# Two transformer layers on one core: gene products of two tiles side by side, two dense steps moved ahead of the experts, and unit-matrix products before the first rows

## The chip, the cores and the metric

The kernel runs on one core of one Trainium2 chip. A core has five engines with a queue of instructions each: TensorE (PE; its weight loads are listed as PEld), VectorE (DVE), ScalarE (ACT), GpSimd (POOL) and SyncE (SP, which here only issues transfers). Within a queue instructions start in order; between queues they wait on semaphores. TensorE writes its products to PSUM, here in banks of 128 partitions by 512 float32; [...] transfers (DMA) move data between SBUF and HBM.

The metric is the time of one execution on the device in microseconds, and of several executions the median.

## The reference

The input x has 4 batches of 512 rows of 256 features, all float32. Two layers follow one another. Each normalises x over the features and adds two branches to it.

Layer 0, branch one, is a linear attention: q, k and v are projections, phi(z) = elu(z) + 1, a running sum over the rows of phi(k) * v is multiplied by phi(q), and a projection closes. Branch two is the gene layer. In short:

```
logits  = (rms_norm(x) * norm_w) @ Wc.T / temperature      # 512 genes per row
w       = softmax of the 32 largest logits
expressed = sum over those 32 of w * genes[index]          # 32 numbers per row
down    = tanh(expressed @ Wd.T);  up = expressed @ Wu.T   # 256 each
branch  = down * rms_norm(x) * up * scale
```

Layer 1, branch one, is an attention with exp(k) weights and running sums over the rows, followed by a gated layer of width 1024. Branch two is a mixture of 16 experts of width 176: two experts are chosen for every row, and a shared gated layer of width 352 is added.

## The kernel before

**Tiles and stages.** A tile is 128 rows; a batch has 4 tiles, all together 16. The stages are written as Python generators, and the helper `together` takes pieces of several of them in turn. The order within the program's queues is then fixed when the program is built: a scheduler goes through the pieces and may move an instruction ahead of others on its engine.

- `layer0(b, i0, nt)` does layer 0 of `nt` tiles of batch b. The batches come as (0; 2 tiles), (0; 2 tiles), (1; 4), (2; 4), (3; 4).
- `mix(b, i0, nt)` does layer 1's attention up to the running sums and the choice of experts.
- `dense(busy)` does the gated layers of layer 1 (width 352 and 1024) for half batches: 8 halves of 11 chunks each, so 88 steps. A step is one `up` (L584, 4 matmuls) and, two steps later, its `down` (L604, 2 matmuls). ScalarE takes a tanh of the gate (`th`, L588), VectorE multiplies (L590, L592). In the first four halves the last multiplication is on GpSimd (L595).
- `route` works out the rows' places per expert, `scatter` sends the 2048 x 2 chosen rows to a buffer in HBM sorted by expert (32 indirect transfers on POOL, L552), `experts` fetches the sorted rows (L720), transposes them (L712), and computes 42 tiles with their expert's weights (L749, L770) in 21 pairs.
- At the end 32 indirect transfers on POOL bring each row's two results back (`ys`, L885), and VectorE adds them to x (L896).

**Dense steps as filling.** 44 of the 88 steps run together with layer 0 and the mixing. Then come 5 with `route`, 14 with `scatter`, a rest before the experts, `run_all(islice(dd, 2 * NC - 19))` with NC = 11, so 3 steps, and the remaining 22 after the experts, together with the gathers. The scatters and gathers carry an extra dependence on the last `down` product written so far (`paced`, `beat`), so that they spread over the dense steps. In the loop after the experts a gather with number `asked` is issued from the step with 5 * asked <= 9 * step on, and an addition with number `added` from 17 * added <= 32 * (step - 3) on.

**The gene branch of a tile** in `layer0`: `logits` (L296, two matmuls of 128x512), a copy to SBUF (L300), `top` on VectorE (four rounds of MAX8 and MATCH_REPLACE, L308 and L309, and the sum L316) which leaves the unscaled weights `e`, and `express`: four transposes of `e` (L323), a copy on ScalarE (`wT`, L325), four matmuls with 32 columns of genes each that write partial sums to four groups of 32 partitions (L328), a copy (`exT`, L329), one matmul with all 128 rows against `wdut`, which holds the weights of down and up four times below one another (L331, result `du`), tanh on ScalarE (L333), one product on VectorE (L336) and four operations on GpSimd (L338 to L341). At the end of `layer0`, `out` projects the attention (L346) and adds it (L349). Every product of `layer0` and `mix` takes one of four PSUM banks in turn (`bank()`).

**The start.** The unit matrix `ident` and `ones` are made on POOL (L107 and L109), transfers bring x of batch 0 and the weights, VectorE multiplies `wct` by `norm_w` (L157) and takes statistics (L208 to L215) and normalised rows (L220). The first products of TensorE are the transposes of these rows (L228).

Of the kernel before, what the change touches and what calls it, by code (L numbers as in the profile page):

```python
# [11 lines left out]
F32 = mybir.dt.float32  # L12
AF = mybir.ActivationFunctionType
ALU = mybir.AluOpType
AX = mybir.AxisListType

P = 128
B, L, D = 4, 512, 256
NT = L // P
NH = D // P  # L20
NG, GD, NACT = 512, 32, 32
NGC = NG // P
# [5 lines left out]
NTT = B * NT  # L28
# [10 lines left out]
def run_all(steps):  # L39
    for _ in steps:  # L40
        pass
# [13 lines left out]
def tile_two_layers(  # L55
# [24 lines left out]
    V, S, G, T = nc.vector, nc.scalar, nc.gpsimd, nc.tensor  # L80
# [12 lines left out]
    def paced(inst):  # L93

        tc.add_manual_dep(
            inst,
            beat[-1],
            mybir.DependencyInfo(mybir.DependencyClass.Sync, mybir.DependencyReason.DATA),
            reason="transfers spread over the dense parts",
        )  # L100
        return inst
# [4 lines left out]
    ident = const.tile([P, P], F32, name="ident")  # L106
    make_identity(nc, ident)  # L107
    ones = const.tile([P, L], F32, name="ones")
    G.memset(ones, 1.0)  # L109

    load_x(0)
    wqkv = wp.tile([P, NH, 3 * D], F32, name="wqkv")
    wct = wp.tile([P, NH, NG], F32, name="wct")
    nc.sync.dma_start(wct, wc.rearrange("(h p) g -> p h g", p=P))
    nwc = wp.tile([P, NH], F32, name="nwc")
# [6 lines left out]
    gn = wp.tile([P, NGC, GD], F32, name="gn")  # L122
    nc.sync.dma_start(gn, genes.rearrange("(c p) k -> p c k", p=P))

    wdut = wp.tile([P, 2 * D], F32, name="wdut")
# [28 lines left out]
    bqkv1 = wp.tile([P, 4], F32, name="bqkv1")  # L154
    V.tensor_scalar(bqkv1, bqkv[:, 0:4], 1.0, None, ALU.add)
    for h in range(NH):
        V.tensor_scalar(wct[:, h], wct[:, h], nwc[:, h : h + 1], None, ALU.mult)  # L157
    rtemp = wp.tile([P, 1], F32, name="rtemp")
    V.tensor_scalar(rtemp, tmp1, 0.1, None, ALU.max)
    V.reciprocal(rtemp, rtemp)  # L160
# [25 lines left out]
    ps_a = ctx.enter_context(tc.tile_pool(name="ps_a", bufs=1, space=bass.MemoryType.PSUM))  # L186
# [5 lines left out]
    io = first.enter_context(tc.tile_pool(name="io0", bufs=2, side="right"))  # L192
    one = first.enter_context(tc.tile_pool(name="one0", bufs=1, side="right"))

    def bank():
        return ps_m.tile([P, L], F32, name="pm")


    carry = wk.tile([P, 6], F32, name="carry")
# [31 lines left out]
    def layer0(b, i0, nt):  # L231
# [56 lines left out]


        rden = io.tile([P, NT], F32, name="rden")  # L290
        exT = one.tile([P, L], F32, name="exT")

        def logits(i):
            pl = bank()
            for h in range(NH):
                T.matmul(  # L296
                    pl, xnT[:, h, i * P : (i + 1) * P], wct[:, h], start=(h == 0), stop=(h == NH - 1)
                )
            lg = io.tile([P, NG], F32, name="lg")
            S.copy(lg, pl)  # L300
            return lg

        def top(i, lg):
            tp = io.tile([P, NACT], F32, name="top")
            rep = io.tile([P, NG], F32, name="rep")
            for r in range(NACT // 8):
                src = lg if r == 0 else rep
                V.max(tp[:, 8 * r : 8 * r + 8], src)  # L308
                V.match_replace(rep, tp[:, 8 * r : 8 * r + 8], src, TAKEN)  # L309
                if r == 0:  # L310
                    nm = io.tile([P, 1], F32, name="nm")
                    V.tensor_scalar(nm, tp[:, 0:1], sl[:, 0, i : i + 1], -1.0, ALU.mult, ALU.mult)
                    e = io.tile([P, NG], F32, name="e")
                    S.activation(e, lg, AF.Exp, bias=nm, scale=sl[:, 0, i : i + 1])
            den = io.tile([P, 1], F32, name="den")
            V.scalar_tensor_tensor(e, rep, TAKEN, e, ALU.is_equal, ALU.mult, accum_out=den)  # L316
            V.reciprocal(rden[:, i : i + 1], den)
            return e

        def express(i, e):  # L320
            pw = bank()
            for c in range(NGC):
                T.transpose(pw[:, c * P : (c + 1) * P], e[:, c * P : (c + 1) * P], ident)  # L323
            wT = io.tile([P, NGC, P], F32, name="wT")
            S.copy(wT.rearrange("p c t -> p (c t)"), pw)  # L325
            px = bank()
            for c in range(NGC):
                T.matmul(px[c * GD : (c + 1) * GD, 0:P], gn[:, c], wT[:, c], start=True, stop=True)  # L328
            S.copy(exT[:, i * P : (i + 1) * P], px[:, 0:P])  # L329
            du = bank()  # L330
            T.matmul(du, exT[:, i * P : (i + 1) * P], wdut, start=True, stop=True)  # L331
            dn = io.tile([P, D], F32, name="dn")
            S.activation(dn, du[:, 0:D], AF.Tanh, scale=rden[:, i : i + 1])  # L333
            cf = io.tile([P, 1], F32, name="cf")
            V.tensor_tensor(cf, rden[:, i : i + 1], sl[:, 1, i : i + 1], ALU.mult)
            V.scalar_tensor_tensor(dn, du[:, D : 2 * D], cf, dn, ALU.mult, ALU.mult)  # L336
            xw = io.tile([P, D], F32, name="xw")
            G.tensor_tensor(xw, xn[:, i], nwb, ALU.mult)  # L338
            G.tensor_tensor(dn, dn, xw, ALU.mult)
            G.tensor_tensor(xs[:, b, i0 + i], xs[:, b, i0 + i], bob, ALU.add)  # L340
            G.tensor_tensor(xs[:, b, i0 + i], xs[:, b, i0 + i], dn, ALU.add)  # L341
# [9 lines left out]

        parts = [lambda h=h, f=f: f(h) for h in range(NH) for f in (attend_kv, attend_q)]
        lg = logits(0)
        for i in range(nt):
            nxt = logits(i + 1) if i + 1 < nt else None
            e = top(i, lg)
            yield
            for part in parts[i * len(parts) // nt : (i + 1) * len(parts) // nt]:
                part()
            yield  # L360
            express(i, e)
            lg = nxt
            yield
        for i in range(nt):
# [206 lines left out]
    NC = len(chunks)  # L571
# [61 lines left out]
    dd = dense(4)  # L633
# [4 lines left out]
    def a(b, i0, nt):  # L638
        return layer0(b, i0, nt), 2 + 4 * nt
# [45 lines left out]
    routing.close()  # L685
    together((scatter(), 33), d(14))

    run_all(islice(dd, 2 * NC - 19))

    held = ctx.enter_context(ExitStack())  # L690
    wx = held.enter_context(tc.tile_pool(name="wx", bufs=2))
# [188 lines left out]
    added = 0  # L880
    for step, _ in enumerate(dd):
        while asked < 2 * NTT and 5 * asked <= 9 * step:
            n, k = divmod(asked, 2)
            paced(
                G.indirect_dma_start(  # L885
                    out=ys[:, asked],
                    out_offset=None,
                    in_=yrows,
                    in_offset=bass.IndirectOffsetOnAxis(ap=slot[:, k, n : n + 1], axis=0),
                ).ins  # L890
            )
            asked += 1
        while added < 2 * NTT and 17 * added <= 32 * (step - 3):
            n, k = divmod(added, 2)
            here = xs[:, n // NT, n % NT]
            V.scalar_tensor_tensor(here, ys[:, added], cpair[:, k, n : n + 1], here, ALU.mult, ALU.add)  # L896
            added += 1
            if added % 4 == 0 and added < 2 * NTT:
                b, i = divmod(n - 1, NT)
                nc.sync.dma_start(  # L900
                    out[b, i * P : (i + 2) * P].rearrange("(t p) d -> p t d", p=P), xs[:, b, i : i + 2]
                )
# [60 lines left out]
```

## Time and profile before

| what | value |
|---|---|
| runs of the kernel | 581.03, 581.01 and 578.38 us, median 581.01 |
| profiled execution, its own time | 576.85 us |
| span of the profiled execution, first to last instruction | 575.1 us |
| mean granted TensorE clock | 0.976 |
| PE busy | 527.4 us (92%) |
| DVE busy | 370.3 us (64%) |
| ACT busy | 228.4 us (40%) |
| POOL busy | 173.6 us (30%) |
| first TensorE product (L228) | 9.32 us |
| last scatter issued (L552), first fetched rows used (L712) | 396.26 us, 401.66 us |
| last VectorE sum of the dense part | 569.70 us |

The page gives shares over the whole span; the stages differ, and what bounds each of them has to be read from that stretch. A matmul in float32 is listed as two records. Records overlap: a record of 128x256 is listed with 0.38 us, but records start 0.216 us apart when nothing hinders them, and it is these starts that count. Idle time in brackets stands before an instruction, with what ended it. A granted clock of 0.5 means that TensorE works at half speed.

### The profile page before, as it was taken

Reading aid. Unit: us, or ns where it says so; the run is one execution under the profiler, and the core shown is the slowest. Engines: PE = TensorE matmul, PEld = TensorE weight load, DVE = VectorE, ACT = ScalarE, POOL = GpSimd, SP = SyncE. Lnnn points to the kernel's source line nnn. Section 1 sums busy time; section 2 is a strip of 40 time slices with the busy share of each in tenths; the row PEclk is TensorE's granted clock in tenths of the full one; section 3 lists DMA queues with packets and bytes.
Section 4 is the critical chain, followed back from the end, with each engine's and each line's share of the span. In section 5 each row is a group of like instructions: output and inputs, shape, how many; then the busy total and the mean of one; then the engine's idle time right before and its main releaser. Section 6 shows DMA issues by size and latency. Waiting matters only on the chain.

```text
span 575.1 us, 7191 instructions
## 1 busy us (share of the span) xinstructions
PE 527.4 (92%) x2324; PEld 383.5 (67%) x2324; DVE 370.3 (64%) x985; ACT 228.4 (40%) x517; POOL 173.6 (30%) x214
## 2 busy tenths in 40 slices
PE   3557989989999999999999989997999999999996
PEld 1344656558656676566677768886677777788885
DVE  4979999998796797967981499232222222236653
ACT  1452746562655825458344611111433333321110
POOL 1235132354222423223352322774000000016660
PEclk9788899999999999999999999999899999999999
DMA  5995000000000000000045630233333332114441
GB/s 165 376 375 206 1 1 0 2 0 1 0 2 0 0 1 2 0 1 1 1 144 158 202 100 11 103 109 126 94 110 101 102 109 92 55 66 129 123 143 40
DMA packets 37736, 46.76 MB, mean 81 GB/s; under 512 B 3936, under 2 KB 34240, under 8 KB 37440
## 3 DMA queue, kind: packets, MB, share of 16 engines
q1 hardware_dynamic: 34624, 37.87, 20.2%
q0 software_dynamic: 3072, 8.39, 4.8%
q8 instruction: 20, 0.33, 0.2%
q14 instruction: 20, 0.16, 0.1%
HBM read 27.64 MB, written 18.61 MB: 80 GB/s over the span
## 4 chain that ended last, share of the span: by engine, by line
PE 54%; DVE 22%; POOL 8%; ACT 7%; issue 4%; DMA 4%; SPq 0%; POOLq 0%; ACTq 0%; DVEq 0%
PE gu L584 12%; PE pu L749 9%; PE acc L604 7%; PE py L770 6%; PE pm L391 5%; DVE rep L309 4%; DVE top L308 4%; POOL xrows L552 3%; PE pt L712 3%; POOL ys L885 3%; PE pm L251 3%; PE pm L296 2%; PE pm L228 2%; PE pm L346 2%; DVE sums L437 2%
## 5 line engine op out<-in xcount | busy, mean ns | idle before, releaser
L584 PE MATMUL gu<-yT,wugt 128*128 128x256 f32 x512 | 126.0, 381 | 0.0
L584 PEld LDWEIGHTS gu<-yT,wugt 128*128 128x128 f32 x512 | 94.9, 190 | 18.9 <-issue 7.2
L588 ACT ACTIVATE th<-gu 128x256 f32<-128x256 f32 (+1 forms) x88 | 33.5, 382 | 122.7 <-PE gu L584 116.1
L885 POOL DMA_INDIRECT ys<-yrows,slot x32 | 30.7, 961 | 133.4 <-PE gu L584 117.9
L604 PE MATMUL acc<-wot,hid 128*128 128x256 f32 x256 | 66.2, 381 | 0.4
L595 POOL TENSOR_TENSOR hid<-hid,th 128x256 f32<-128x256 f32 (+1 forms) x44 | 34.1, 779 | 101.2 <-ACT hid L594 97.9
L590 DVE SCALAR_TENSOR_TENSOR th<-th,gu 128x256 f32<-128x256 f32 (+1 forms) x88 | 36.1, 412 | 41.6 <-ACT th L588 41.5
L749 PE MATMUL pu<-wex,xgT 128*128 x168 | 58.3, 470 | 0.8 <-DMA xg<-xrows 0.8
L604 PEld LDWEIGHTS acc<-wot,hid 128*128 128x128 f32 x256 | 48.1, 190 | 9.3 <-POOL hid L595 2.0
L251 PE MATMUL pm<-xnT,wqkv 128*128 128x512 f32 (+1 forms) x120 | 46.7, 530 | 3.9 <-ACT qk L398 1.7
L584 PE MATMUL gu<-xn1T,sgu 128*128 128x256 f32 (+1 forms) x192 | 47.3, 382 | 1.4 <-ACT hid L594 1.3
L758 DVE TENSOR_TENSOR hb<-pu,hb 128x176 f32<-128x176 f32 x42 | 14.3, 341 | 51.9 <-ACT hb L757 51.9
L391 PE MATMUL pm<-w,xn1T 128*128 128x512 f32 (+1 forms) x128 | 45.9, 502 | 0.1
L584 PEld LDWEIGHTS gu<-xn1T,sgu 128*128 128x128 f32 (+1 forms) x192 | 33.8, 181 | 9.5 <-ACT hid L594 2.6
L770 PE MATMUL py<-wex,hgT 128*128 x168 | 39.8, 379 | 0.0
L391 PEld LDWEIGHTS pm<-w,xn1T 128*128 128x128 f32 x128 | 24.7, 194 | 21.7 <-issue 17.5
L251 PEld LDWEIGHTS pm<-xnT,wqkv 128*128 128x128 f32 x120 | 23.8, 201 | 21.9 <-issue 13.2
L770 PEld LDWEIGHTS py<-wex,hgT 128*128 128x128 f32 x168 | 31.8, 190 | 7.9 <-issue 0.4
L552 POOL DMA_INDIRECT xrows<-xn,slot x32 | 30.9, 966 | 19.7 <-DVE th L590 10.3
L749 PEld LDWEIGHTS pu<-wex,xgT 128*128 128x128 f32 x168 | 29.4, 195 | 10.5 <-ACT xgT L726 1.2
L762 DVE COPY hgT<-pt 128x512 f32<-128x512 f32 x21 | 14.5, 691 | 30.0 <-PE pt L712 30.0
L296 PE MATMUL pm<-wct,xnT 128*128 128x512 f32 x64 | 33.4, 659 | 0.3 <-ACT xnT L244 0.2
(163 smaller groups left out, 872.2 us busy)
## 6 DMA issues: line engine op xcount, KB each, us to landing
xrows<-zero SPq DMA_DIRECT2D x1, 6016.0 KB, 23.3
wex<-in_w_gate_up_dram SPq DMA_DIRECT2D x8, 704.0 KB, 4.7
xg<-xrows SPq DMA_DIRECT2D x21, 256.0 KB, 2.7
yrows<-yg SPq DMA_DIRECT2D x21, 256.0 KB, 2.1
xs<-in_x_dram SPq DMA_DIRECT2D x4, 512.0 KB, 8.0
wugt<-in_wug_dram SPq DMA_DIRECT2D x1, 2048.0 KB, 11.9
wex<-in_w_down_dram SPq DMA_DIRECT2D x4, 512.0 KB, 4.8
out_dram<-xs SPq DMA_DIRECT2D x7, 256.0 KB, 2.8
```

Source lines behind the costliest of these rows:

```text
L251: T.matmul(pm, wqkv[:, h, c * P : (c + 1) * P], xnT[:, h, 0:W], start=(h == 0), stop=(h == NH - 1),)
L296: T.matmul(pl, xnT[:, h, i * P : (i + 1) * P], wct[:, h], start=(h == 0), stop=(h == NH - 1))
L391: T.matmul(o[:, 0:n], xnT[:, h, i * P : (i + 1) * P], w1[:, h, at : at + n], start=(h == 0), stop=(h == NH - 1),)
L552: sc = G.indirect_dma_start(out=xrows, out_offset=bass.IndirectOffsetOnAxis(ap=slot[:, k, i : i + 1], axis=0), in_=xn1[:, i // NT, i % NT] ...
L584: T.matmul(gu[0:m, k], w[:, h, at : at + m], ins[which][:, h], start=(h == 0), stop=(h == NH - 1))
L588: S.activation(th[0:m], gu[0:m, 0], AF.Tanh, scale=0.5)
L590: V.scalar_tensor_tensor(th[0:m], th[0:m], 1.0, gu[0:m, 0], ALU.add, ALU.mult)
L595: G.tensor_tensor(hid[0:m], hid[0:m], th[0:m], ALU.mult)
L604: mm = T.matmul(acc[:, t], hid[0:m, t * P : (t + 1) * P], dw[0:m, dc], start=(n == 0 and t == 0), stop=(n == NC - 1), skip_group_check=True,)
L749: T.matmul(pg[:, 0 : 2 * NI], xT[:, i, h], wex[:, bass.ds(at[i] + h * 2 * NI, 2 * NI)], start=(h == 0), stop=(h == NH - 1),)
L770: mm = T.matmul(py[:, i * D : (i + 1) * D], hT[:, i, h], wex[:, bass.ds(at[i] + EW - (2 - h) * D, D)], start=(h == 0), stop=(h == 1),)
L885: G.indirect_dma_start(out=ys[:, asked], out_offset=None, in_=yrows, in_offset=bass.IndirectOffsetOnAxis(ap=slot[:, k, n : n + 1], axis=0) ...
```

## The change

There are five edits, and a number in the tail that goes with one of them.

1. **Gene products in pairs.** `express` is cut into three. `turn_genes(e)` transposes and copies the weights of a tile. After every second tile `express(i, wTs)` multiplies both tiles' weights with the genes: the first tile takes two groups of 32 partitions, the second the other two, and each group adds up two chunks of genes (8 matmuls for the pair, as before). One copy takes the result of both. Then two matmuls follow, one for each tile, each with half of the 128 rows and a bank of its own. `expressed` is the part behind them, once per tile.
2. **Dense steps.** `2 * NC - 17` takes the place of `2 * NC - 19`: five steps run between scatters and experts, and 20 remain behind the experts. For those, 15 takes the place of 17 in the condition for an addition.
3. **Unit-matrix products.** Sixteen products of `ident` with itself are put at the head of TensorE's queue. They write to the bank of the dense sums, and nothing reads them.
4. **`ones`** is filled by VectorE, not by GpSimd.
5. **`wct`** is multiplied by `norm_w` on GpSimd, not on VectorE.

```diff
-    G.memset(ones, 1.0)
+    V.memset(ones, 1.0)
...
-        V.tensor_scalar(wct[:, h], wct[:, h], nwc[:, h : h + 1], None, ALU.mult)
+        G.tensor_scalar(wct[:, h], wct[:, h], nwc[:, h : h + 1], None, ALU.mult)
...
+    idle = ps_a.tile([P, 2, D], F32, name="acc")
+    for _ in range(16):
+        T.matmul(idle[:, 0, 0:P], ident, ident, start=True, stop=True)
...
-        exT = one.tile([P, L], F32, name="exT")
...
-        def express(i, e):
+        def turn_genes(e):
             pw = bank()
             for c in range(NGC):
                 T.transpose(pw[:, c * P : (c + 1) * P], e[:, c * P : (c + 1) * P], ident)
             wT = io.tile([P, NGC, P], F32, name="wT")
             S.copy(wT.rearrange("p c t -> p (c t)"), pw)
+            return wT
+
+        def express(i, wTs):
             px = bank()
-            for c in range(NGC):
-                T.matmul(px[c * GD : (c + 1) * GD, 0:P], gn[:, c], wT[:, c], start=True, stop=True)
-            S.copy(exT[:, i * P : (i + 1) * P], px[:, 0:P])
-            du = bank()
-            T.matmul(du, exT[:, i * P : (i + 1) * P], wdut, start=True, stop=True)
+            for c in range(2):
+                for g in range(NGC):
+                    j = g % 2 * 2 + c
+                    T.matmul(
+                        px[g * GD : (g + 1) * GD, 0:P], gn[:, j], wTs[g // 2][:, j], start=(c == 0), stop=(c == 1)
+                    )
+            exT = io.tile([P, P], F32, name="exT")
+            S.copy(exT, px[:, 0:P])
+            dus = [bank(), bank()]
+            for t, du in enumerate(dus):
+                half = slice(t * P // 2, (t + 1) * P // 2)
+                T.matmul(du, exT[half], wdut[half], start=True, stop=True)
+            for t, du in enumerate(dus):
+                expressed(i + t, du)
+
+        def expressed(i, du):
             dn = io.tile([P, D], F32, name="dn")
...
+        wTs = []
         for i in range(nt):
...
-            express(i, e)
+            wTs.append(turn_genes(e))
+            if len(wTs) == 2:
+                express(i - 1, wTs)
+                wTs = []
...
-    run_all(islice(dd, 2 * NC - 19))
+    run_all(islice(dd, 2 * NC - 17))
...
-        while added < 2 * NTT and 17 * added <= 32 * (step - 3):
+        while added < 2 * NTT and 15 * added <= 32 * (step - 3):
```

## The prediction

> **What bounds the kernel now.** I read four views: the page for the whole, the busy times by stretch, the waits of each engine, and the timeline around the places that the diff touches. The page first: busy tenths of the two busiest engines and the granted TensorE clock, in 40 slices of 14.4 us.
>
> ```profile
> PE 527.4 (92%) x2324; PEld 383.5 (67%) x2324; DVE 370.3 (64%) x985; ACT 228.4 (40%) x517; POOL 173.6 (30%) x214
> ...
> PE   3557989989999999999999989997999999999996
> ...
> DVE  4979999998796797967981499232222222236653
> ...
> PEclk9788899999999999999999999999899999999999
> ```
>
> TensorE (PE) is full from the fifth slice on, with one dip in slices 27 and 28. Before that VectorE (DVE) is the full one. The busy times by stretch (length, then busy us of PE, PEld, DVE, ACT, POOL, granted clock) put numbers on it:
>
> ```profile
> 14.92:54.16 39.24, 25.76 (x92) 15.52 (x90) 34.73 (x109) 15.62 (x33) 15.43 (x21) 0.78 0.97 350
> 54.16:86.00 31.84, 26.16 (x116) 16.59 (x116) 31.38 (x97) 19.31 (x44) 6.31 (x10) 0.95 0.00 1
> 86.00:141.00 55.00, 53.08 (x231) 34.27 (x231) 53.87 (x146) 30.59 (x67) 23.64 (x30) 1.00 0.00 1
> 141.00:224.70 83.70, 81.20 (x363) 56.21 (x362) 68.25 (x174) 45.01 (x99) 24.77 (x31) 1.00 0.00 1
> 224.70:297.50 72.80, 70.80 (x303) 46.99 (x302) 62.13 (x156) 37.54 (x87) 25.27 (x27) 1.00 0.02 6
> ...
> 397.68:407.13 9.45, 4.89 (x14) 3.25 (x14) 0.94 (x3) 2.21 (x4) 0.00 (x0) 0.64 0.52 153
> ```
>
> Until 54 us DVE is busy 34.7 of 39.2 us and TensorE runs at 0.78 of its clock; to 86 us DVE is the bound; to 141 us both are; from there to 297 us PE is, with some 4.5 us idle. The 9.45 us from 397.68 are the one hole. The timeline of that seam between scatters and experts (start, us, engine):
>
> ```profile
> 396.82 1.03 PE L604 MATMUL acc<-wot,hid 128*128 128x256 f32 x4
> ...
> 398.81 8.65 SPq L720 DMA_DIRECT2D xg<-xrows  x6
> ...
> 401.66 1.09 PE L712 MATMUL pt<-ident,xg 128*128 128x128 f32 x4 [3.81 <-DMA xg<-xrows]
> 402.86 0.58 ACT L726 COPY xgT<-pt 128x512 f32<-128x512 f32 x1 [5.46 <-PE pt L712]
> 403.46 1.28 ACT L757 ACT_TABLE_LOAD   x1
> ...
> 403.50 2.71 PE L749 MATMUL pu<-wex,xgT 128*128 x4 [0.75 <-DMA xg<-xrows]
> ```
>
> The last dense product streams until 397.68, the expert's rows arrive at 401.66, and the work behind that runs at half clock. Last, the gene products of one tile in the PE timeline (L328 genes, L331 down and up), and where DVE starts in earnest:
>
> ```profile
> 98.10 0.43 PE L328 MATMUL pm<-wT,gn 128*32 128x128 f32 x8
> 98.46 0.70 PE L584 MATMUL gu<-yT,wugt 128*128 128x256 f32 x2
> 98.99 1.04 PE L331 MATMUL pm<-wdut,exT 128*128 128x512 f32 x2
> ...
> 14.92 0.69 DVE L308 MAX8 top<-lg 128x8 f32<-128x512 f32 x1 [2.88 <-ACT lg L300]
> ```
>
> [...] the four column tiles of L328: they start within 0.02 us of each other (278.595 to 278.615), and some 0.09 us pass unused on either side. No row tile is in this trace. [...] 0.5 is recorded from 400.30 to 407.13, and transposes start 0.213 us apart instead of 0.109.
>
> **Seam and tail.** Two dense steps go from behind the experts to before them. A step is 12 records 0.216 us apart, 2.59 us; two are 5.18. Their operands are ready, and they add no transfer. They run from 397.68 to 402.86, over the 3.98 us of idle; that the experts then start 1.2 us after their rows costs nothing, as the same 5.18 us are gone from the tail. Gain 3.98. The clock also stays up: eight transposes give back 8 x 0.104 = 0.83 us and four L749 records 4 x 0.291 = 1.16, some 2.0. I give back 0.4, because the 1.28 us table load behind the copy at 402.86 then ends after the first L749 pair instead of under it. Seam: -5.6 (ends -4.0, idle alone, and -6.0).
>
> In the tail 20 steps remain, with gathers asked at the old rate (9 in 5 steps) and additions faster (32 in 15 steps, not 17). The last gather is asked at step 18 as before, but its addition, formerly at step 20 of 22, now also belongs to step 18 of 20, and the built order of DVE ends: th of step 19, last addition, hid of step 19. Call E the end of the down product of step 16. In the trace the last gather starts 0.27 us after it (560.17, 560.44), and its addition 2.88 us later (563.32): E+3.15. Hid then ends at E+3.97, and the last down product starts near E+4.05; unhindered it would start after up(19), down(17) and down(18), at E+3.29. Tail: +0.75 (0.4 to 1.5). A gather 1 us slower adds 1 us. Earlier additions wait too, but hid has a step to spare there.
>
> **Front.** Sixteen unit-matrix products, 32 records, start once the unit matrix is made (near 1.9 us; the mask on POOL ends at 1.79). Cold they take 32 x 0.213 = 6.8 us, to 8.7, before the first rows are wanted (9.32): they cost nothing. If the clock rises, the first four transposes take 0.44 instead of 1.14 us and the first pair of logits products (four records) 1.73 instead of 3.4. The two products on wct leave DVE (0.88 us at 6.55), but DVE still waits for the temperature until 7.97, so only some 0.35 us come of it. On POOL they are bounded by twice its memset of 128x512 (2 x 0.53) and four times a 128x256 TENSOR_TENSOR (4 x 0.73); [...] wct and norm_w have landed by 6.4 us, so POOL ends by 7.5 to 9.4, and the logits start near 10: hidden by that transpose and copy. Each us later would delay all logits by one. The memset of ones costs DVE nothing, idle until 4.32. So the first MAX8 starts near 12.6 instead of 14.92: 2.3 us.
>
> How much lasts? From 14.92 to 54.16 DVE idles 4.5 us: 1.94 and 0.36 for tanh, 0.87 for phi, 0.91 for POOL. In the built order the two gene tails come late, behind statistics of the next batches, whose x lands at 31.7 and 33.2 us: about 1.2 us of new waiting, then 1.7 for POOL, which has both tiles' four operations in a row. That leaves 1.2 us saved, so up to 3.5 in all. I take -2.5 (ends 0, if those waits eat it, and -4.5).
>
> **Gene products.** Per pair of tiles before: two column blocks of 0.45 us and two L331 products of 2 x 0.43: 0.9 + 1.73. After: one block of eight matmuls, four rounds, about 0.69 us if whole; the built order splits five of the eight into 2 and 6 (drained twice, about 1.12). Over the six pairs of the dense stages, four split, that is a loss of about 0.5 us. The two L347 products take half the rows each and a bank each: 0.86 + 0.19 us of drain if side by side, saving 0.68 a pair, 4.1 in six; 1.73 + 0.19 if in turn, losing 1.1. One exT copy of 0.27 us a pair leaves ACT and one of two waits for it leaves PE, some 0.8 us in all. Side by side this is -4.4, in turn +0.8 to +1.6. Where DVE is bound as well (to 141 us) it is worth less: I take -2.5.
>
> **Sum.** -5.6 + 0.75 - 2.5 - 2.5 = -9.85 us on a profiled execution of 576.85 (span 575.1 and 1.75 around it): 567.0. The median of the runs shown, 581.01, lies 4.2 us above that execution; I carry this offset over: 571.2.
>
> **The rivals.** (1) Only the dense move counts: row tiles go in turn or PE waits for DVE, and the front's gain is lost in DVE's order. Then -5.6 + 0.75 gives 576.2. For it: DVE is 98% busy from 54 to 141 us. Against: the 2.88 us before the first MAX8 are plain PE time. (2) The change does not do what it says at the tail: gathers slower than 2.88 us hold the last hid, and what the seam won returns. At 4 us more, with rival 1, 580.2. Against: the last five gathers reached their addition in 2.78 to 2.91 us. (3) Slower: a pair needs three of the four banks together, each du held until DVE's dn has read it, and PE, in order, stands at the second L347 with projections and dense products queued behind it; DVE waits for those in turn. It decides from about 1.2 us a pair (8 pairs, 9.85); at 1.7 us it gives 584.8. For it: dn stood behind other DVE work for up to 2.3 us (281.10 to 283.40). Against: PE waited for dn only twice in 30 to 345 us, 1.9 us.
>
> **How the numbers follow.** About 0.5%, 2.9 us, is what a measurement tells from no change. All parts as reckoned: 0.62, 571.2, its own range 568 to 574. More than that, near 567: 0.06. Rival 1: 0.20, 576.2. Rival 2: 0.06. Rival 3: 0.06. Faster takes the first two and nearly all of rival 1, 0.86; within 0.5% rival 2 and the rest, 0.08; slower 0.06. The range of 8 in 10 runs from 566 (both part gains at their ends) to 577 (rival 1 and some noise).
>
> **What would show it.** Right: PE without a gap before the first pt, clock 1.0 there; L347 records of a pair starting within 0.02 us, du block near 1.05; first MAX8 near 12.6; last hid waiting for a gather, PE idle under 1 us. Wrong: L347 records 0.43 us apart for all four; PE idle before the second of a pair or before the last acc; logits waiting for POOL. The forecast fails most easily in the front and the genes, whose PE time may turn into waiting for DVE.

## The result, and the profile after

The changed kernel took 575.82 us in the median (573.79 to 577.93), against 580.15 us for the kernel before (578.38 to 581.52) in the same set of runs: a ratio of 0.9931, with a 95% interval of 0.9913 to 0.9948. That is 4.3 us, where the forecast had 9.85. The profiled execution has a span of 573.6 us.

The page of the changed kernel, the rows that answer to those shown of before:

```profile
PE 530.2 (92%) x2356; PEld 388.5 (68%) x2356; DVE 368.4 (64%) x984; ACT 226.6 (40%) x509; POOL 173.3 (30%) x215
...
PE   8547899989999999999999989879999999999995
...
DVE  6969999998896897968952687223322222225553
...
PEclk9767999999999999999999999979999999999998
```

Before, the dip of PE stood in slice 28 (7 tenths; the prediction put it at 27 and 28). It is gone, and a new one stands in slices 26 and 27, with the granted clock down in slice 27. The seam itself is as forecast, in the PE timeline of the changed kernel (start, us, engine):

```profile
404.97 1.03 PE L628 MATMUL acc<-wot,hid 128*128 128x256 f32 x4
405.83 0.60 PE L736 MATMUL pt<-ident,xg 128*128 128x128 f32 x4
407.19 1.16 PE L773 MATMUL pu<-wex,xgT 128*128 x3 [0.75 <-ACT xgT L750]
```

No gap stands ahead of L736, and its four transposes, one record each, take 0.60 us in place of 1.09. But they start at 405.83 us, 4.2 us later than before, although two steps of 2.59 us ahead of them account for 5.2 and the first scatter came 5.3 us earlier. The time went between the first and the last scatter: 39.4 us in the first profile of the kernel before (356.89 to 396.26), 44.7 in this one (351.58 to 396.26). The waits of the changed kernel from 352 to 400 us show where (waiting instruction, what ended it, us in total, times, longest):

```profile
ACT th L612 <- PE acc L628: 8.7, 2, 5.3
...
PEld acc L628 <- DVE xs L639: 6.0, 1, 6.0
PE acc L628 <- DVE xs L639: 5.6, 1, 5.6
ACT th L612 <- remote: 5.0, 2, 3.9
```

ScalarE's tanh is late by several us in the middle of the scatters; VectorE, which needs it, and then TensorE stand. The same list for the first profile of the kernel before has no wait of PE at all there. I call this the hold: ScalarE's tanh comes late again and again among the scatters, and the other engines wait behind it. The question was then whether the change makes it.

### The profile page after: what moved, and what is told of

The parts are those of the page before. It is cut to its first block, busy times and chain, and to the rows that moved or that the text cites. A ratio compares the mean times of both kernels' runs of the same rounds, so it can differ in the third digit from the quotient of the medians.

```text
span 573.6 us, 7243 instructions
## 1 busy us (share of the span) xinstructions
PE 530.2 (92%) x2356; PEld 388.5 (68%) x2356; DVE 368.4 (64%) x984; ACT 226.6 (40%) x509; POOL 173.3 (30%) x215
## 4 chain that ended last, share of the span: by engine, by line
PE 48%; DVE 27%; issue 8%; POOL 6%; DMA 4%; ACT 4%; SPq 1%; POOLq 0%; another core or an unknown queue 0%; ACTq 0%; DVEq 0%
PE gu L608 11%; PE pu L773 9%; PE py L794 6%; PE acc L628 6%; POOL ys L909 5%; DVE rep L313 5%; DVE top L312 4%; PE pm L415 4%; PE pt L736 3%; DVE sums L461 3%; DMA wot<-in_wout_dram 2%; DVE sums L452 2%; PE pm L256 2%; PE pm L233 2%; DVE th L614 2%
## 5 line engine op out<-in xcount | busy, mean ns | idle before, releaser
L608 PEld LDWEIGHTS gu<-yT,wugt 128*128 128x128 f32 x512 | 96.2, 192 | 20.9 <-issue 8.8
L773 PE MATMUL pu<-wex,xgT 128*128 x168 | 56.9, 461 | 0.8 <-ACT xgT L750 0.8
L773 PEld LDWEIGHTS pu<-wex,xgT 128*128 128x128 f32 x168 | 28.6, 190 | 10.1 <-ACT xgT L750 1.0
L618 ACT COPY hid<-gu 128x256 f32<-128x256 f32 (+1 forms) x44 | 16.4, 373 | 42.4 <-DVE th L614 42.0
```

What stands on the lines that cost most here:

```text
L608: T.matmul(gu[0:m, k], w[:, h, at : at + m], ins[which][:, h], start=(h == 0), stop=(h == NH - 1))
L773: T.matmul(pg[:, 0 : 2 * NI], xT[:, i, h], wex[:, bass.ds(at[i] + h * 2 * NI, 2 * NI)], start=(h == 0), stop=(h == NH - 1),)
```

## The experiments

A set of runs stays on one chip and has runs of the kernel before in it. The sets turned out to be of two kinds, so that each is named by its chip: on A the kernel before took 580.26 us, on B 576.76 and 576.91 (two sets), on C 576.21, on D 576.22.

### Both kernels once more (chip A)

Both kernels are unchanged.

> The changed kernel once more, for a second profile. In its first profile the 32 scatters took 44.7 us from the first start to the last (39.4 in the kernel before), with the tensor engine idle for about 5.6 us in between, and that ate the 5.3 us which were won ahead of them. Theory 'the stall belongs to the order of work': it is there again, at the same scatters, 44 to 45 us, and the span is again about 573.6. Theory 'the stall is a chance event of one execution': the scatters take 39.4 to 39.7 us, and the span is 568 to 569 in this profile; the median of the timed runs is then made up of executions with and without it.

> The kernel before once more, for a second profile. Its first profile took 576.85 us by its own time, less than any of its 11 timed runs (578.38 to 581.52). Theory 'the first profile was a lucky execution': this one is about 580 by its own time, and some stage of it, the scatters being the first suspect, is 2 to 4 us longer than in the first. Theory 'profiled executions are as a rule shorter than timed ones': again about 577.

Measured: the changed kernel 575.64 us, ratio 0.9914 (0.9886 to 0.9942); the kernel before 581.09 us in its profiled execution. The kernel before has the hold too: 43.8 us from first to last scatter, as the changed kernel has (43.7). Its ScalarE timeline, second profile:

```profile
365.74 0.38 ACT L588 ACTIVATE th<-gu 128x256 f32<-128x256 f32 x1 [2.21 <-issue]
371.63 0.38 ACT L588 ACTIVATE th<-gu 128x256 f32<-128x256 f32 x1 [5.51 <-PE gu L584]
...
386.11 0.38 ACT L588 ACTIVATE th<-gu 128x256 f32<-128x256 f32 x1 [6.00 <-PE acc L604]
393.88 0.94 ACT L588 ACTIVATE th<-gu 128x256 f32<-128x256 f32 x3 [7.39 <-remote]
```

and its PE timeline:

```profile
388.43 1.89 PE L584 MATMUL gu<-yT,wugt 128*128 128x256 f32 x8
395.23 2.08 PE L604 MATMUL acc<-wot,hid 128*128 128x256 f32 x4 [4.92 <-DVE hid L592]
```

An undisturbed step has its tanh every 2.59 us (2.21 of idle). Here single ones come after 5.9, 6.4 and 7.8 us, and TensorE stands for 4.92 us shortly before the last scatters. At the seam it then has no gap: the late dense steps fill the time until the expert's rows are there. So the change does not make the hold, and it was the first profile of the kernel before that had none. The theory "chance event of one execution" falls as well: the hold is there in every profile from this chip.

### Dense move undone, genes undone (chip A)

```diff
-    run_all(islice(dd, 2 * NC - 17))
+    run_all(islice(dd, 2 * NC - 19))
...
-        while added < 2 * NTT and 15 * added <= 32 * (step - 3):
+        while added < 2 * NTT and 17 * added <= 32 * (step - 3):
```

> The changed kernel with the dense move undone (17 steps are left behind the experts in place of 15, two fewer ahead of the first rows; the adds again at 17). My forecast prices the move at -5.6 at the seam and +0.75 in the tail, so this should be slower than the changed kernel by about 4.9 us (3.4 to 5.6): about 580.7. If the seam's idle is no longer there, because the stage ahead ends later for another reason, it is within 1.5 us of the changed kernel.

Measured: 576.78 us, ratio 0.9953 (0.9935 to 0.9970), about 1.1 us over the changed kernel of the same set, as the second branch of the expectation has it. The first rows are used 3.9 us earlier than in the changed kernel (402.24 against 406.16) and the end comes 0.5 us later (span 574.7 against 574.2): what two steps more ahead of the experts cost there, they give back behind. With the hold there is hardly a gap for them to fill: even without them TensorE waits for only 0.60 us ahead of the first transposes.

For the genes, `express`, `exT` and the loop are taken from the kernel before:

```diff
-            wTs.append(turn_genes(e))
-            if len(wTs) == 2:
-                express(i - 1, wTs)
-                wTs = []
+            express(i, e)
```

> The changed kernel with the gene products one tile at a time, as before. Forecast: the pairs are worth 2.5 us (4.4 if they run side by side), so this is 578.3 to 580.2. The milestones of the changed kernel's trace (third stage of the first layer 2.2 us earlier, fourth 1.9) say 4 us, so 579.8. If what is won there is lost again in the scatters, then it is 575.8, and its scatters take less than 44.7 us.

Measured: 578.87 us, ratio 0.9990 (0.9963 to 1.0017), 3.2 us over the changed kernel. Its runs spread from 576.23 to 583.87 us, four of the twelve above 581.7, so the 3.2 is rough. The last theory of that expectation falls: the time is not 575.8, and the scatters take 43.9 us, no less than the changed kernel's 43.7 on this chip.

### Single parts, and the scatters (chip B)

First the dense move alone, on the kernel before; its diff is the one above, turned round.

> The kernel before with the dense move alone (two more steps ahead of the first rows, adds at 15). My forecast: -5.6 at the seam and +0.75 in the tail, -4.85, so 575.3 against a median of 580.2. New theory, from the second profile of the kernel before: as a rule the tensor engine is held for 4 to 5.6 us in the middle of the scatters, which leaves nothing to fill at the seam (gap ahead of the first rows under 0.8 us, not 4); then the move is worth -1.0 as in the changed kernel (0 to -1.5): 579.2, and the profile shows the hold near the 12th scatter and no gap at the seam.

Measured: 571.14 us against 576.76, ratio 0.9904 (0.9887 to 0.9921). On this chip no profile has the hold: the scatters take 39.4 us. The old forecast held (-4.85; measured -5.6 in the medians), the new theory, which made the hold a rule, did not.

```diff
-    V.memset(ones, 1.0)
+    G.memset(ones, 1.0)
...
-        G.tensor_scalar(wct[:, h], wct[:, h], nwc[:, h : h + 1], None, ALU.mult)
+        V.tensor_scalar(wct[:, h], wct[:, h], nwc[:, h : h + 1], None, ALU.mult)
...
-    idle = ps_a.tile([P, 2, D], F32, name="acc")
-    for _ in range(16):
-        T.matmul(idle[:, 0, 0:P], ident, ident, start=True, stop=True)
```

> The changed kernel with its front undone: no unit-matrix products, ones set on GpSimd, wct scaled on the vector engine. Forecast: the front is worth 2.5 us (0 to 4.5), so 578.3. From the profiles (at the first scatter the changed kernel with genes one by one is 1.6 us ahead of the kernel before): 577.4. From the sum of what the other two undone parts cost (1.0 and 3.0 of 4.3): only 0.3, so 576.1.

Measured: 569.47 us, ratio 0.9869 (0.9849 to 0.9889). The expected figures in us belong to a kernel before of 580.2 and do not fit here; against the changed kernel on the same chip (567.41, next set) taking the front away costs 2.1 us, or 1.7 by the ratios, whose intervals just overlap.

In the next kernel 24 of the 32 scatters are left out, so that those rows of the experts' input stay zero:

```diff
             for i in range(NTT):
+                if k * NTT + i >= 8:
+                    yield
+                    continue
                 sc = G.indirect_dma_start(
```

> The changed kernel with 24 of its 32 scatters left out (those rows of the expert input stay zero, and the output is wrong by that). If the scatters cause the hold of the activation engine, which in every disturbed profile begins when the 10th scatter starts: the steps of the dense part run every 2.59 us from 350 to 400, the tensor engine has no gap over 1 us there, and the end is 4 to 6 us earlier (568 to 570). If it comes from the dense part itself, from instruction loading or from the recording: a hold of about 5.6 us near 371 as before.

Measured: span 565.4 us, no hold. Without a hold on this chip to begin with, it says nothing of its cause. It does say that without a hold the scatters no longer bound the changed kernel: with a quarter of them the time from the first scatter to the end is 213.6 us, with all of them 213.1.

And the scatters laid over 17 steps:

```diff
-    together((scatter(), 33), d(14))
+    together((scatter(), 33), d(17))
...
-    run_all(islice(dd, 2 * NC - 17))
+    run_all(islice(dd, 2 * NC - 20))
```

> The changed kernel with the 32 scatters spread over 17 dense steps in place of 14, and as many steps ahead of the experts in all (three fewer between the last scatter and the first rows). A scatter comes every 1.38 us in place of 1.26. If the hold comes from the rate at which the scatters are issued, it shrinks, and PE's gap goes to the seam: 573 to 576. If it comes after a number of scatters, whatever their rate: it is there again at the 10th to 12th, and with it the scatters end 3 us later, which opens a gap of up to 3 us at the seam: 576 to 579.

Measured: 568.10 us, ratio 0.9854 (0.9835 to 0.9872); the last scatter starts 39.9 us after the first in place of 39.5, and no gap opens. The edit hardly did what was expected of it: in the trace the scatters from the second to the 16th still start 1.26 to 1.27 us apart, and the later ones 1.26 and 1.33 in turn, where 1.38 was expected. So nothing is learnt of the hold, and this version could not have told a rate from a number at the 10th scatter even where the hold is.

### The changed kernel without the hold (chip B again)

> The changed kernel once more. In the runs so far the kernel before took 580.2 wherever the profiles had the hold among the scatters, and 576.8 where they had none, and its first profile (576.85) had none. So: if the kernel before takes about 576.8 here, no hold, the last scatter near 391.2, and the changed kernel is 8.7 us faster (front 1.2 to 2.5, genes 2 to 3, dense move 5.6 less 0.5): 567 to 569. If it takes about 580.2 here, the hold is there and the changed kernel is again at 575 to 576.5.

Measured: 567.41 us (566.61 to 567.83) against 576.91, ratio 0.9840 (0.9822 to 0.9857), so 9.5 us faster. The stretch from 370 to 380 us (length, busy us of PE, PEld, DVE, ACT, POOL, granted clock), in this profile of the changed kernel:

```profile
370.00:380.00 10.00, 10.00 (x48) 8.64 (x47) 3.64 (x9) 1.53 (x4) 7.63 (x8) 1.00 0.30 105
```

and in the first one, with the hold:

```profile
370.00:380.00 10.00, 4.42 (x13) 3.26 (x12) 3.13 (x7) 1.15 (x3) 6.13 (x7) 0.73 0.23 79
```

TensorE is busy all the time in the one, for 4.42 of 10 us and at 0.73 of its clock in the other. It is the same program.

> The kernel before with the dense move alone, once more. Where the kernel before takes 580.2 (the hold is there): 579.2, the move worth -1.0 (0 to -1.5), where my forecast said -4.85 and the run with a kernel before of 576.8 gave -5.6. Where it takes 576.8: again -5.6.

Measured: 571.25 us, ratio 0.9910 (0.9892 to 0.9927): 5.2 us faster in ratio, as without the hold before.

> The changed kernel with the scatters spread over 17 steps, once more. Where the kernel before takes 580.2: if the hold depends on the rate of the scatters, 572 to 574, less than the changed kernel; if it comes after ten scatters whatever the rate, 575 to 578. Where it takes 576.8: the same as the changed kernel within 1 us.

Measured: 567.80 us, ratio 0.9852 (0.9832 to 0.9873), the same as the changed kernel.

In the next kernel every second scatter is left out:

```diff
             for i in range(NTT):
+                if i % 2:
+                    yield
+                    continue
                 sc = G.indirect_dma_start(
```

> The changed kernel with every second scatter left out (those rows of the expert input stay zero, and the output is wrong by that), so that 16 are issued, about one in 2.6 us. Where the kernel before takes 580.2: if what holds the activation engine fills up at the rate of the scatters and drains in between, no hold at all; if it is a number of scatters, the hold begins at the 10th of these, about 24 us after the first. Where it takes 576.8: no hold, and nothing is learnt.

Measured: span 565.1 us, no hold on this chip.

### The parts once more (chip C)

> The changed kernel with the dense move undone, once more. Where the kernel before takes 576.8 (no hold among the scatters): the move is worth 4.85 by my forecast, 5.6 by its run alone, so 567.4 + 4.9 to 5.6 = 572.3 to 573.0, and the gap ahead of the first rows is back (about 4 us). Where it takes 580.2: 1 us over the changed kernel, as in its first run.

Measured: 573.58 us, ratio 0.9951 (0.9935 to 0.9967), so 6.4 us of the 9.2 that the changed kernel's ratio gives on this kernel before go with the dense move, somewhat more than the 4.9 to 5.6 expected. The gap is back, in the PE timeline of this kernel:

```profile
392.55 1.03 PE L628 MATMUL acc<-wot,hid 128*128 128x256 f32 x4
397.54 1.08 PE L736 MATMUL pt<-ident,xg 128*128 128x128 f32 x4 [3.97 <-DMA xg<-xrows]
399.38 2.71 PE L773 MATMUL pu<-wex,xgT 128*128 x4 [0.75 <-DMA xg<-xrows]
```

and the changed kernel without the hold, in the same view:

```profile
397.33 1.03 PE L628 MATMUL acc<-wot,hid 128*128 128x256 f32 x4
398.20 0.60 PE L736 MATMUL pt<-ident,xg 128*128 128x128 f32 x4
399.55 1.45 PE L773 MATMUL pu<-wex,xgT 128*128 x4 [0.75 <-ACT xgT L750]
```

This is the forecast's seam line by line: 3.97 us of idle gone, transposes 0.60 in place of 1.08 us, four L773 records 1.45 in place of 2.71. The granted clock is 1.00 from 390 to 410 us, where without the dense move it is 0.79 to 400 us and 0.87 from there.

> The changed kernel with the gene products one tile at a time, once more. Without the hold: forecast 2.5, so 569.9; by the gap between the runs of the changed kernel (-9.5) and what the front undone (2.1) and the dense move (4.9 to 5.6) leave: 1.8 to 2.5, so 569.2 to 569.9. With the hold: 3.0 over the changed kernel, as in its first run.

Measured: 571.07 us, ratio 0.9917 (0.9891 to 0.9942), 4.4 us over the changed kernel by the ratios (0.9917 less 0.9840). Expected were 1.8 to 2.5. At the first scatter the profile lies 2.1 us behind the changed kernel (354.31 against 352.24); another 2.0 us come in the tail, where a gather is late, VectorE's sum with it, and PE waits for the bank:

```profile
PE acc L609 <- DVE xs L620: 2.2, 1, 2.2
```

That wait (2.1 us on chip A) is 0.38 us in the changed kernel's third profile.

> The changed kernel with the scatters over 17 steps, for a third time. Where the kernel before takes 580.2: if the hold depends on the rate, 572 to 574; if not, 575 to 578. Without the hold it is the changed kernel within 1 us (two runs so far: 568.1 and 567.8 against 567.4).

Measured: 568.04 us, ratio 0.9857 (0.9833 to 0.9880). Three runs of this version have given the changed kernel's time; it is not a better one.

> The changed kernel with every second scatter left out, once more (the output is wrong by those rows). Where the kernel before takes 580.2: if what holds the activation engine fills up at the rate of the scatters and drains in between, no hold; if it is a number of scatters, the hold begins at the 10th of these, about 24 us after the first. Without the hold nothing is learnt.

Measured: span 564.7 us, no hold here either.

### More unit-matrix products (chip D)

```diff
-    for _ in range(16):
+    for _ in range(26):
```

> The changed kernel with 26 unit-matrix products in place of 16. The 16 end 0.6 to 2.0 us before the first transpose, and in three of ten profiles the tensor engine's clock was halved for 3.4 us from 10.4 to 10.6 on, with the first MAX8 near 14.6 in place of 12.6. Ten more products of 0.11 us (at the full clock) bridge that. If the front's worth hangs on the clock there: the first MAX8 always near 12.6 to 13.2, and 0.3 to 0.7 us less in the median, ratio 0.983 where the kernel before takes 576.8. If the lost time is made up by the end of the first stage anyway (there the same profiles were 2.2 to 2.4 us ahead, as the others): no difference, ratio 0.984 (0.9925 where the kernel before takes 580.2).

Measured: 570.64 us, ratio 0.9898 (0.9880 to 0.9916), so about 3.3 us slower than the changed kernel; both expectations missed. In the first profile of the changed kernel the records of these products come to start 0.111 us apart, and a product is two records: by that ten more take some 2.2 us, where the expectation has 0.11 a product. The first MAX8 is at 13.52 us, a little above the 12.6 to 13.2 of the first expectation, and then 3 us are lost in ScalarE's queue. Its timeline in this kernel:

```profile
23.52 0.59 ACT L329 COPY wT<-pm 128x512 f32<-128x512 f32 x1 [4.15 <-PE pm L327]
30.00 0.63 ACT L672 ACTIVATE wot<-wot 128x512 f32<-128x512 f32 x1 [5.90 <-DMA wot<-in_wout_dram]
30.54 0.46 ACT L269 ACTIVATE phi<-pm,nbqk 128x256 f32<-128x256 f32 x1
```

and in the changed kernel, third profile:

```profile
22.85 0.59 ACT L329 COPY wT<-pm 128x512 f32<-128x512 f32 x1 [4.15 <-PE pm L327]
24.56 0.47 ACT L269 ACTIVATE phi<-pm,nbqk 128x256 f32<-128x256 f32 x1 [1.12 <-PE pm L256]
25.07 0.42 ACT L270 ACTIVATE phi<-phi 128x256 f32<-128x256 f32 x1
29.04 0.63 ACT L672 ACTIVATE wot<-wot 128x512 f32<-128x512 f32 x1 [3.55 <-DMA wot<-in_wout_dram]
```

The built order of ScalarE differs: with ten products more on another engine, the scheduler put the scaling of `wot` (L672), which waits for a transfer until 29 to 30 us, ahead of a `phi` (L269) that the changed kernel starts at 24.56. VectorE waited 4.46 us for that `phi`. So this run is no measure of the clock at 10.5 us. The second run over 17 steps (chip B) is a better one: its first MAX8 was at 14.60, and its first scatter at 352.05, no later than in the changed kernel (352.24).

> The changed kernel with every second scatter left out, for a third time (the output is wrong by those rows). Where the kernel before takes 580.2: if what holds the activation engine fills up at the rate of the scatters and drains in between, no hold; if it is a number of scatters, the hold begins at the 10th of these. Where it takes 576.8: no hold, as in its first two runs, and nothing is learnt.

Measured: span 565.8 us, no hold. Whether the hold needs a number or a rate of scatters was not decided, as none of these runs met the hold.

## Why the prediction was right and wrong

The table gives, from the profiles, the start of the first scatter and the time from there to the end, in us. The first column of times holds the front and the genes, the second the scatters, seam and tail.

| kernel | chip | first scatter | from there to the end |
|---|---|---|---|
| before, first profile | not recorded, no hold | 356.89 | 218.24 |
| dense move alone, two profiles | B | 354.52, 355.69 | 213.36, 213.36 |
| changed, dense move undone | C | 352.63 | 218.23 |
| changed, genes undone | C | 354.31 | 215.16 |
| changed, front undone | B | 354.91 | 213.24 |
| changed | B | 352.24 | 213.13 |
| before, second profile | A, hold | 356.70 | 222.58 |
| changed, two profiles | not recorded and A, hold | 351.58, 352.24 | 222.02, 221.99 |
| changed, dense move undone | A, hold | 352.48 | 222.25 |
| changed, genes undone | A, hold | 355.15 | 222.70 |

**Front, -2.5: the size is borne out in part, the way to it is not.** Taken out of the changed kernel, the front costs 2.1 us in the medians and 2.7 at the first scatter (354.91 against 352.24). With the genes one by one it brings less: the first scatter is at 354.31 and 355.15, against 354.52 to 356.89 in the four profiles without front and pairs, and the median is no better than that of the dense move alone (ratio 0.9917 against 0.9904 and 0.9910), as the tail then takes 2 us longer. The first MAX8 came at 12.25, 12.60 and 12.85 us in the three profiles of the changed kernel (forecast 12.6). But this lead does not last. The MAX8 of the third tile starts at 53.50 us in the changed kernel and at 53.69 with the front undone; only the fifth tile's is apart:

```profile
84.06 0.68 DVE L312 MAX8 top<-lg 128x8 f32<-128x512 f32 x1
```

in the changed kernel, third profile, and

```profile
85.85 0.68 DVE L309 MAX8 top<-lg 128x8 f32<-128x512 f32 x1
```

with the front undone. And three runs whose first MAX8 was as late as 14.60 to 14.87 us (8 of the 32 scatters, the second over 17 steps, the second with every second scatter) have their first scatter at 351.6 to 352.1 all the same. So the forecast's 2.3 us ahead of the first MAX8 are not what is won at the end, and its -2.5 comes near by luck. Undoing the front also changes the built order of VectorE and ScalarE (as the 26 products did); whether the 2 us come from that, no run here separates.

One price was outside its bounds: a product on `wct` takes some 1.59 us on POOL (two 3.18), above the upper end of 2 x 1.46. The second ended at 9.81 us, 0.4 us ahead of the logits (10.24), which had to await ScalarE's copy until 10.14 anyway, and so cost nothing, as forecast.

**Gene products, -2.5: the mechanism right, the size not separable.** Taken out of the changed kernel they cost 2.1 us at the first scatter (354.31 against 352.24), and more in all (4.4 on chip C, 3.2 on chip A). Added with the front undone, they bring 1.7 us in the medians (569.47 against 571.14 and 571.25), and a first scatter at 354.91, against 354.52 to 356.89 without. So their worth runs from 1.7 to 4.4 us, with what else is in the kernel. That two row tiles would run side by side was my estimate, which no trace of the kernel before shows; the prediction's "drain" is my name for the 0.09 us unused on either side of L328, and its 0.19 is about twice that. The row tiles do run side by side, in the PE timeline of the changed kernel's third profile:

```profile
198.57 0.94 PE L339 MATMUL pm<-wT,gn 128*32 128x128 f32 x16
199.44 0.70 PE L608 MATMUL gu<-yT,wugt 128*128 128x256 f32 x2
200.07 1.13 PE L347 MATMUL pm<-wdut,exT 64*128 64x512 f32 x4
201.13 1.13 PE L608 MATMUL gu<-yT,wugt 128*128 128x256 f32 x4
```

Two tiles' down and up take 1.06 us (200.07 to 201.13), where one tile took 0.86 and the forecast had 1.05 for the pair; the records of a pair start 0.007 us apart (forecast: within 0.02). The other 2 us that undoing the genes costs in the tail were not in my sum; there a gather comes late at the end of a half batch, as shown above.

Front and genes together are the safer figure: the two medians of the dense move alone (571.14 and 571.25) less the changed kernel's 567.41 leave 3.7 to 3.8 us, where the forecast had 5.0. The parts do not add up: each alone brings the first scatter about 1 us ahead, on the average of the few profiles, and both together some 3.7.

**Seam and tail, -5.6 + 0.75 = -4.85: right without the hold, worth nothing with it.** From the first scatter to the end the dense move alone takes 218.24 to 213.36, -4.88 us in both profiles. Of the tail's 0.75 the trace shows a wait of 0.55 us for the last hid. On chip A the same stretch is 222.0 to 222.7 us in all four kernels: no edit moves it by more than 0.7. Amid the scatters TensorE stands idle there for 4.1 to 5.8 us in all, in the kernel before too, and its clock is halved for 3.4 to 6.8 us besides. In the changed kernel the first transposes come 53.9 us after the first scatter in place of 46.0. In the kernel before it is 50.2 in place of 44.8: of TensorE's delay, 3.8 us fall into the wait for the first rows that was there anyway. So to the end the hold costs the changed kernel 8.9 us (222.0 less 213.1) and the kernel before 4.3 (222.58 less 218.24), and the difference, 4.5, is most of what the two steps gain without it. The gap that two steps were to fill does not exist in these executions.

**The sum: near for the execution it was made on, with some luck.** From the first profile of before to the third of the changed kernel the span falls from 575.1 to 565.4, by 9.8 us, against 9.85 forecast; the medians on chip B differ by 9.5. In the medians the dense move alone brings 5.6 and 5.7 where 4.85 was forecast, front and genes 3.7 to 3.8 where 5.0 was: two errors that nearly cancel.

**The step that failed** is the carrying over: "The median of the runs shown, 581.01, lies 4.2 us above that execution; I carry this offset over". That carries over the sum too, with its seam of -5.6: the prediction put at nothing, without a reason, that the runs might lack the wait which the two steps fill. The offset was no constant. The profiled execution took 576.85 us, which is what the kernel before takes without the hold (576.2 to 576.9), and the three runs shown, all above it by 1.5 to 4.2 us, were of the other kind, as their times say (the hold itself was seen in its second profile). Which chip that profile and those runs were made on is not recorded; in every later set the profile was of the same kind as the runs beside it. A gap of that size between a profile and every run beside it means that something in the runs is not in the profile, and what it is may lie where the change acts. I had the two numbers and took the difference for noise around the kernel. Of the forecast for the runs, the -4.85 of seam and tail measured about -1.1 (576.78 against 575.64), and front and genes about -3.5 (580.26 to 576.78) where -5.0 was forecast: 4.3 to 4.6 us in all in place of 9.85.

**The rivals.** Rival 1 gave 576.2, near the measured 575.8, with the parts the wrong way round: it kept the dense move and gave up front and genes. Rival 2 and rival 3 did not occur: in the changed kernel's third profile gathers did not hold the end beyond 0.55 us, and PE shows no wait before a second L347.

## What to carry to other kernels

Before a sum is made on one profile, compare that execution's own time with every run beside it; if it lies outside them, ask which stage could differ, and take a second profile before carrying the sum over. A gain that consists of filling a gap lasts only in executions that have the gap: look at whether another stall, earlier in the same stage, would close it. And an edit to one engine's queue can reorder another's: after each one, read the built order of the engines that wait for transfers. For the same reason a part taken out of the changed kernel and the same part added to the old one need not give the same number: measure both.

## What the runs showed of the hardware

**The hold.** On chip A, and in the first profile of the changed kernel, ScalarE's tanh comes late although TensorE's product for it is listed as done (the tanh at 370.72 below has its product listed until 365.56). VectorE's multiplication follows each late tanh at once (at 365.47, 371.13 and 375.42 us in the second profile of the changed kernel, 0.03 to 0.04 us after the tanh has ended), so it is ScalarE that is late. In all five profiles the first late one was due just as the 10th scatter starts (368.33 and 368.33 us, 363.20 and 363.22, 363.87 and 363.88, 364.10 and 364.13, 366.77 and 366.83), and it came 1.2 us late in four, 3.3 in one. As dense steps and scatters run in step, this is also always the same dense step; no run with the hold tells the two apart. The timeline of the changed kernel's second profile:

```profile
363.88 0.96 POOL L576 DMA_INDIRECT xrows<-xn,slot  x1 [0.30 <-issue]
...
365.05 0.38 ACT L612 ACTIVATE th<-gu 128x256 f32<-128x256 f32 x1 [3.39 <-PE acc L628]
...
370.72 0.38 ACT L612 ACTIVATE th<-gu 128x256 f32<-128x256 f32 x1 [5.28 <-PE acc L628]
...
375.00 0.38 ACT L612 ACTIVATE th<-gu 128x256 f32<-128x256 f32 x1 [3.90 <-remote]
...
377.18 1.22 PE L628 MATMUL acc<-sdn,hid 128*128 128x256 f32 x2 [5.58 <-DVE xs L639]
```

In the same profiles many landings of transfers are missing from the record. The page then gives no time to landing for any transfer that shares a semaphore with one of them. Of the early transfer that clears the buffer of sorted rows, its list has, in the second profile of the kernel before,

```profile
xrows<-zero SPq DMA_DIRECT2D x1, 6016.0 KB
```

and in the third profile of the changed kernel, which has no hold,

```profile
xrows<-zero SPq DMA_DIRECT2D x1, 6016.0 KB, 23.4
```

Counted in the traces, the landings up to the first scatter are all there with the hold too (688 records), and so are those between scatters and gathers (672). They are missing in the two stages with indirect transfers: among the scatters 153 to 196 records are left of 512, from the first gather on 243 to 276 of 656. The loss begins within 5 us of the first scatter, while the first late tanh was due 11.6 us after it. Among the gathers too single tanhs are late (4.3 us of idle before one in the second profile of the kernel before, where 2.2 is undisturbed). With records missing, the names behind the arrows in these profiles ("issue", "remote", "PE acc") are uncertain as well.

Why ScalarE is late, and why landings are missing, no run here shows. Whether one brings about the other, or both come from the chip or what is around it, stays open. What can be said is that both go together in all profiles, five with and fifteen without, and that the timed runs of those sets are longer too (the kernel before took 580.15 and 580.26 us there, 576.21 to 576.91 elsewhere).

**The clock at the start.** In four of the fourteen profiles with sixteen unit-matrix products TensorE's clock was halved again at 10.45 to 10.77 us, for 3.4 us (the expectation above counted three of ten), although the products had raised it (in the first profile of the changed kernel their records start 0.213 us apart until 5.86 us and 0.111 from 6.06 on). The pause between the last product and the first transpose does not sort them: it is 0.8 to 1.3 us in these four and 0.6 to 2.0 in the others. When the clock rose does: at 7.04 to 7.35 us in the four, at 5.09 to 6.60 or 7.48 to 7.87 in the ten. Why, no run here shows. It moved the first MAX8 by 2 us (14.60 to 14.87 in place of 12.25 to 12.85), and in the run over 17 steps nothing at the first scatter.
